# The first feed-forward block's up product as seven half-size products in one PSUM bank, with all places found anew

## The chip, the core and the metric

The kernel runs on one core of a Trainium2 chip. The metric is device time in microseconds (us) of one execution, the median of several runs. A core has five engines with a queue each, which run their own instructions in order and wait for one another by semaphores: TensorE (PE in the profile; PEld is its weight load), VectorE (DVE), ScalarE (ACT), GpSimd (POOL) and SyncE (SP), which here issues the DMAs. Matmuls read SBUF and write PSUM, which has eight banks.

## The reference, cut to what matters

For each of 64 graphs with 256 nodes and 256 features (all float32), a transformer layer on the graph is followed by two graph-attention layers and a second feed-forward block:

```python
# layer 0
x = ln(src + masked_attention(src) @ Wo + bo, g1, beta1)       # 8 heads
ff = gelu(x @ W1 + b1) @ W2 + b2                                # 256 -> 1024 -> 256: block "ffa"
x = ln(x + ff, g2, beta2)
# layer 1
h = gat(gat(x, adj, gW1, ga1), adj, gW2, ga2)
h = ln(x + h, g_ln1, b_ln1)
ff = relu(h @ w_ff1 + b_ff1) @ w_ff2 + b_ff2                    # block "ffb"
out = ln(h + ff, g_ln2, b_ln2)
```

The change concerns `x @ W1`, the up product of block `ffa`.

## The kernel before

All weights stay in SBUF. The work of one graph is cut into 210 named operations, each a method that emits one or a few instructions. A table `PLACES` gives each name a place in time, and graph g's operation stands at `g * PERIOD + place`; all operations of all graphs are emitted in the order of these places, under a schedule by hand that keeps this order on each engine:

```python
plan += [(g * PERIOD + t, i, ops[n]) for i, (n, t) in enumerate(PLACES.items())]
with tc.manual_schedule():
    for _, _, f in sorted(plan, key=lambda p: p[:2]):
        f()
```

The places only set an order; the engines run as fast as their waits allow. A graph's operations reach over more than five periods, so in the steady state up to six graphs are in work at once, and each engine goes through the same cycle of operations for each graph. `LOAD_PLACES` and the constants after it place the weights' loads and one-time preparations in the same order. Both tables come from a planner outside the kernel, of which only the places are here.

Names used below. `qk0`, `qk1`, `s0`, `s1`, `vp1` to `vp7`, `po0`, `po1`, `wo` are TensorE's products of attention (queries and keys, scores, values as seven half-size products, heads, output); `max`, `exp`, `rec`, `nrm`, `eT`, `pm` with two digits are softmax, transposition and masking of a half and a head; `qkc`, `oT`, `vc1` are ScalarE's copies out of PSUM; `va` VectorE's sums. `ga`, `ip`, `h1`, `h2` are TensorE's products of the graph attention; `gac`, `z`, `ze`, `zd`, `h1c` ScalarE's part (copy, scores, exponential, division, copy) and `zl`, `zm`, `zx`, `h2a` VectorE's (leaky step, mask, maximum, last add), with A or B for the two layers. `st`, `rt`, `nb`, `ln` and `lg`, `lb` are the layer norms: statistics on VectorE, root and offset on GpSimd, application on ScalarE, gain and shift on GpSimd. `tg` and `te` are one-column activations on ScalarE that bring the Gelu or the Exp table in.

A feed-forward block has the letter a or b: `aT`, `aW`, `aR` transpose the input in 32x32 squares on VectorE, write it to DRAM and read it back, the features then on the partitions; `au0` to `au3` (method `up`, line 408) each make 256 of the 1024 hidden features in one PSUM bank, four matmuls of 128x128 weights and 256 nodes:

```python
for f in range(f0, f0 + 2):
    for k in range(KD):
        nc.tensor.matmul(p[:, f - f0, :], self.wa[:, k, f * P:(f + 1) * P], self.x.nodes(k),
                         start=(k == 0), stop=(k == KD - 1))
```

`ax0` to `ax3` (method `act`, line 416) apply the function on ScalarE, two instructions each, from PSUM to SBUF. The down product is made of seven half-size products `ad1` to `ad7` (line 442) already, from differences `aS1` to `aS4` on GpSimd (line 431), summed up on VectorE by `ae`, `ae1`, `ae5`, `ae6`, `ae7` (line 450). `ag`, `ar` prepare the residual on GpSimd. Block b is alike and keeps its form.

PSUM is split into a pool `mm` of three banks that serves every product named above but the scores (four banks) and part of the down products (one bank).

TensorE's order in one period, from the graph attention's first product on:

```
ga1 ga0 bd2 ipA bd1 bd5 bd3 au3 bd6 bd4 au1 au0 h11 h10 au2 ipB bd7 s1 po0 ad3 ad2 ad5 ad1 vp1 ad4 ad7 h2
vp6 ad6 qk0 po1 vp7 vp2 wo vp5 qk1 vp4 s0 vp3 bu0 bu1 bu2 bu3
```

Of the kernel before, what the change touches and what calls it, by code (L numbers as in the profile page):

```python
# [9 lines left out]
F32 = mybir.dt.float32  # L10
# [5 lines left out]
ALU = mybir.AluOpType  # L16
AX = mybir.AxisListType

P = 128
S = 32  # L20
# [4 lines left out]

PERIOD = 46.817006
PLACES = {
    "te": 58.6001, "load": 103.4118, "xT": 107.5511, "qk0": 114.6030, "qkc0": 118.3668, "chk": 120.8735,  # L30
    "qk1": 124.1765, "qkc1": 125.7661, "s0": 125.8575, "max01": 128.7295, "max00": 129.3509, "exp00": 129.7832,
    "exp01": 131.1121, "max03": 131.1181, "rec00": 132.0400, "max02": 134.4535, "nrm00": 135.2195, "exp03": 135.2725,
    "exp02": 135.4496, "xS": 137.4219, "rec03": 139.9573, "rec01": 140.4767, "cast": 142.2696, "eT00": 146.3076,
    "nrm03": 146.9438, "rec02": 148.2727, "s1": 150.9705, "eT03": 153.2280, "eW00": 153.8592, "max10": 154.0476,
    "max12": 154.0810, "nrm01": 155.8608, "vp1": 157.2562, "eT01": 157.4751, "max11": 157.8791, "eW03": 157.8980,
    "exp10": 158.1195, "exp12": 158.3273, "rec10": 158.3689, "vc1": 159.1149, "nrm10": 159.7013, "exp11": 159.7336,
    "vp6": 160.5405, "y": 161.0091, "eR03": 162.4098, "jT": 162.4105, "va6": 163.4204, "eW01": 164.7326,
    "eT10": 167.2105, "vp7": 167.6555, "max13": 167.6890, "rec11": 168.1740, "rec12": 168.2052, "vp2": 170.1442,
    "va1": 170.6120, "va7": 170.6882, "nrm11": 170.8368, "vp5": 170.8550, "eW10": 171.9961, "exp13": 172.1818,
    "nrm12": 172.1818, "vp4": 172.3252, "nrm02": 172.3767, "rec13": 172.4280, "vb1": 172.4717, "nrm13": 172.8764,  # L40
    "va9": 173.2360, "vp3": 174.4288, "va5": 174.7560, "eT12": 175.2182, "eR00": 175.4819, "eT02": 175.4846,
    "va3": 175.9229, "va4": 176.3211, "eW02": 177.5999, "yb": 178.0406, "eT13": 179.1841, "eR01": 179.5795,
    "eT11": 181.3423, "eW12": 184.6438, "pm01": 187.1564, "pm03": 187.6323, "eR02": 190.0912, "eW11": 190.1738,
    "pm02": 191.4548, "vb0": 191.5291, "pm00": 196.1306, "eR12": 196.9971, "po0": 198.3305, "tg": 198.9884,
    "oT0": 203.0869, "pm12": 203.1747, "eW13": 203.2324, "eR11": 203.2324, "pm11": 204.4851, "eR10": 204.7143,
    "pm10": 205.0782, "eR13": 206.0478, "pm13": 210.8288, "po1": 212.8636, "oT1": 213.1603, "wo": 217.3657,
    "ya": 217.7482, "st1": 218.9733, "rt1": 219.6991, "nb1": 220.2046, "ln1": 221.5003, "aT": 223.1218,
    "aW": 223.5752, "aR": 228.4507, "au3": 233.0381, "au1": 235.4781, "ax3": 235.8335, "au0": 237.9132,
    "ax1": 237.9558, "ag": 239.9088, "ax0": 240.5771, "ar": 242.0854, "au2": 242.5252, "aS1": 243.4701,
    "ax2": 244.9981, "ad3": 245.3069, "aS2": 246.6456, "aS3": 246.8135, "ad2": 248.2816, "aS4": 248.9901,  # L50
    "ad5": 249.6928, "ad1": 250.8660, "ad4": 251.3076, "ad7": 251.4266, "ae": 251.5139, "ae1": 251.8960,
    "ae7": 253.0074, "ad6": 254.7553, "ae5": 256.3794, "ae6": 256.8974, "st2": 258.4200, "rt2": 261.8668,
    "nb2": 262.3317, "ln2": 262.5757, "lg2": 265.0579, "lb2": 265.2601, "hT": 266.8520, "hW": 269.2569,
    "hR": 270.2281, "no": 270.8009, "ga1": 272.1110, "gac1": 272.1189, "ga0": 272.2913, "gac0": 272.3261,
    "ipA": 275.0907, "zA": 275.3493, "zlA": 276.2527, "zmA": 279.1628, "zxA": 279.3183, "zeA": 279.6032,
    "zdA": 282.9918, "h11": 287.2020, "h10": 288.5186, "h1c0": 289.7363, "h1c1": 289.7594, "ipB": 290.9252,
    "zB": 291.0511, "zlB": 291.2329, "zmB": 292.8115, "zxB": 293.7145, "zeB": 297.0297, "zdB": 298.0214,
    "h2": 298.5319, "h2a": 302.0194, "st3": 302.9618, "rt3": 303.6799, "nb3": 304.4826, "ln3": 305.0823,
    "bT": 307.2531, "bW": 308.3438, "bR": 314.8880, "bu0": 316.1573, "bu1": 316.7829, "bx0": 316.9660,
    "bu2": 317.2893, "bx1": 317.6215, "bu3": 317.8128, "bx2": 318.1921, "bx3": 319.0641, "bS1": 319.5718,  # L60
    "bg": 319.6424, "bS2": 319.9853, "br": 320.8440, "bd2": 321.4268, "bd1": 322.8462, "bS4": 323.7921,
    "bS3": 324.5246, "bd5": 325.8209, "bd3": 325.8217, "bd6": 327.2744, "bd4": 327.8256, "be1": 328.2453,
    "be5": 329.8795, "be6": 331.7955, "be": 332.7084, "bd7": 337.7800, "be7": 342.4869, "st4": 344.9883,
    "rt4": 345.1762, "nb4": 348.7424, "ln4": 355.9706, "lg4": 361.3841, "lb4": 362.9841, "store": 364.6106,
}
LOAD_PLACES = [
    101.366, 142.216, 210.928, 179.882, 111.464, 161.951, 112.848, 100.995, 176.282, 144.653, 176.020, 153.991,
    122.933, 161.019, 117.691, 142.137, 176.282, 109.079, 176.294, 241.513, 253.083, 121.392, 182.287, 196.253,
    207.821, 129.075, 215.004, 184.114, 158.647, 204.480, 111.464, 207.869, 213.180, 214.956, 213.949, 222.383,
    259.685, 196.355, 250.874, 266.888, 159.287, 109.005, 208.310, 182.294, 221.373, 230.689, 234.043, 257.548,  # L70
    184.117,
]
V_PLACE, OUT_PLACE, FFA_PLACE, GAT_PLACE, FFB_PLACE, ODD_PLACE = 113.801, 158.647, 184.117, 225.125, 272.083, 240.000

# [11 lines left out]
def binary_graphs(  # L88
# [13 lines left out]
    nc = tc.nc  # L102
    B, N, D = x.shape
    R = 2
    FF = W1.shape[1]
    H = 8
    DH = D // H
    KD = D // P
    KF = FF // P
    C = N // P  # L110
# [15 lines left out]
    def mm_tile(shape, name, dt=F32):  # L126
        return ps_mm.tile(shape, dt, tag="mm", name=name)
# [42 lines left out]
    def rowvec(v, n, name):  # L170
        t = const.tile([P, n], F32, name=name)
        loads.append((t, _row(v, n)))
        return t
# [39 lines left out]
    wo, bo_r = weight(Wo, "wo"), rowvec(bo, D, "bo_r")  # L213
# [5 lines left out]
    g1_c, be1_c = mixed_vec(g1, "g1_c"), mixed_vec(beta1, "be1_c")  # L219
    w2, b2_r = weight(W2, "w2"), rowvec(b2, D, "b2_r")  # L220
    w2_t, f2_t = (const.tile([P, 3, KF // 2, P], F32, name=f"{n}_t") for n in ("w2", "f2"))
    g2_r, be2_r = rowvec(g2, D, "g2_r"), rowvec(beta2, D, "be2_r")
    gw = bp.tile([P, 2, KD, D], F32, tag="ff", name="gw", bufs=3)
    gw1 = gw[:, 0]
# [16 lines left out]
    def ffn_weights(w, b, gain, shift, row, shift_row, name, wb, wb_t):  # L241


        p = mm_tile([P, KF], f"{name}_b_ps")
        for f in range(KF):
            for k in range(KD):
                nc.tensor.matmul(p[:, f:f + 1], w[:, k, f * P:(f + 1) * P], shift[:, k],
                                 start=(k == 0), stop=(k == KD - 1))
        nc.vector.tensor_tensor(b, p, b, ALU.add)
        for k in range(KD):  # L250
            nc.scalar.activation(w[:, k], w[:, k], AF.Copy, scale=gain[:, k])
        nc.vector.tensor_tensor(row, row, shift_row, ALU.add)
        seven[name] = seven_weights([[wb[:, h * KF // 2:(h + 1) * KF // 2, d * P:(d + 1) * P] for d in range(2)]
                                     for h in range(2)], [wb_t[:, i] for i in range(3)])

    seven = {}

    def seven_weights(b, t):

# [126 lines left out]
    class Ffn:  # L386


        def __init__(self, wa, ba, func, wb, gain, row, name):
            self.wa, self.ba, self.func, self.wb, self.name = wa, ba, func, wb, name  # L390
            self.h, self.p = {}, {}
            self.gain, self.row = gain, row
            self.x = Transposed(f"{name}_T", bp, "sT", 2)
            self.ps = {}
            self.t = None

        def residual(self, src):
            self.r = bp.tile([P, C, D], F32, tag="res", name=f"{self.name}_res", bufs=3)
# [12 lines left out]
        def act(self, f0):  # L411
            half, f1 = divmod(f0, KF // 2)
            if half not in self.h:
                self.h[half] = bp.tile([P, KF // 2, N], F32, tag="ff", name=f"{self.name}_h{half}", bufs=3)
            for f in range(2):
                nc.scalar.activation(self.h[half][:, f1 + f, :], self.ps[f0][:, f, :], self.func,  # L416
                                     bias=self.ba[:, f0 + f:f0 + f + 1])

        def hidden(self, c, half):

# [31 lines left out]
    class Graph:  # L452
# [244 lines left out]
        def operations(self):  # L697
# [38 lines left out]
            for n, f, src in (("a", self.ffa, lambda: self.y), ("b", self.ffb, lambda: self.ffa.r)):  # L736
                ops[f"{n}T"] = lambda f=f, src=src: f.x.squares(src())
                ops[f"{n}W"], ops[f"{n}R"] = f.x.write, f.x.read
                ops[f"{n}g"] = lambda f=f, src=src: f.residual(src())
                ops[f"{n}r"] = f.residual_row  # L740
                for i in range(KF // 2):
                    ops[f"{n}u{i}"] = lambda f=f, i=i: f.up(2 * i)
                    ops[f"{n}x{i}"] = lambda f=f, i=i: f.act(2 * i)
                for i in range(1, 5):
# [303 lines left out]
```

## Time and profile before

| | |
|---|---|
| median of 3 runs | 3187.36 us (3186.81 to 3187.7) |
| the profiled execution: its time | 3185.44 us |
| its span, first to last instruction | 3183.7 us |
| TensorE matmul busy | 3076.2 us, 97% of the span |
| VectorE, ScalarE, GpSimd busy | 2377.3, 2328.3, 2196.3 us |
| up product of `ffa` (L408) | 2048 records, 475.8 us |
| its Gelus (L416) | 512, mean 473 ns, 214.8 us |
| down product's 128-wide matmuls, largest group (L442) | 1024 records, 139.6 us |
| mean granted clock of TensorE | 0.987 |

Busy time of a group is the time in which at least one of its instructions ran, so overlapping matmuls are not counted twice. A float32 matmul leaves two records. In a timeline a row gives start, length, engine, line, operation, `out<-in`, tile, shape and count, and in brackets the idle time of the engine before it with what ended it.

### The profile page before, as it was taken

The numbers are of one execution on the slowest core, as the hardware profiler recorded it, in microseconds if no ns is written. First come the engines' busy times: TensorE is split into PE (matmuls) and PEld (weight loads), VectorE is DVE, ScalarE is ACT, GpSimd is POOL, SyncE is SP. The second block draws the span as 40 slices with busy tenths as digits, with TensorE's granted clock in tenths as the row PEclk, the third lists the DMA queues.
The fourth block names the chain that finished last, engine by engine and source line by source line (L and its number), as shares of the span: only waits on it lengthen the run. The fifth ranks groups of instructions, "written<-read, shape, count | busy, mean of one in ns | idle before, by whom it ended". The sixth has DMA issues, their size and how long they took to land. (4 is left out here: it accounts for less than half of the span.)

```text
span 3183.7 us, 63717 instructions
## 1 busy us (share of the span) xinstructions
PE 3076.2 (97%) x21725; PEld 2588.3 (81%) x21725; DVE 2377.3 (75%) x5153; ACT 2328.3 (73%) x6599; POOL 2196.3 (69%) x2630
## 2 busy tenths in 40 slices
PE   6999999999999999999999999999999999999995
PEld 4788888888888888888888888888888888888784
DVE  5777777777777777777777777777777777777742
ACT  5777777777777777777777777777777777777742
POOL 2477677677677677677677677677677677677664
PEclk8999999999999999999999999999999999999997
DMA  7555455455455455555455455455455455455421
GB/s 207 155 151 144 141 156 144 140 156 145 140 156 144 140 156 145 140 156 145 140 156 145 140 155 146 140 153 148 140 154 147 139 154 147 139 154 148 133 70 31
DMA packets 808331, 456.62 MB, mean 143 GB/s; under 512 B 334528, under 2 KB 717376, under 8 KB 808000
## 3 DMA queue, kind: packets, MB, share of 16 engines
q1 hardware_dynamic: 808000, 452.49, 49.5%
q8 instruction: 174, 2.85, 0.4%
q14 instruction: 157, 1.29, 0.1%
HBM read 242.63 MB, written 201.33 MB: 139 GB/s over the span
## 5 line engine op out<-in xcount | busy, mean ns | idle before, releaser
L568 ACT ACTIVATE e<-e,rden 128x256 f32<-128x256 f32 x1024 | 455.8, 504 | 87.5 <-DVE rden L563 87.5
L408 PE MATMUL ffb_ps<-ffb_T,f 128*128 128x256 f32 x2048 | 461.6, 384 | 25.6 <-DMA ffb_T<-ffb_T_d 23.2
L408 PE MATMUL ffa_ps<-ffa_T,w 128*128 128x256 f32 x2048 | 475.8, 381 | 0.0
L558 ACT ACTIVATE e<-s,nmax 128x256 f32<-128x256 f32 x1024 | 470.0, 469 | 7.5 <-DVE nmax L550 6.9
L408 PEld LDWEIGHTS ffb_ps<-ffb_T,f 128*128 128x128 f32 x2048 | 392.8, 193 | 84.7 <-DMA ffb_T<-ffb_T_d 20.6
L577 DVE TENSOR_TENSOR pm<-eT,adT 128x512 f32<-128x512 f32 x512 | 436.7, 854 | 3.1 <-DMA eT<-eT_d 3.1
L326 DVE STREAM_TRANSPOSE eT_sq<-e 128x512 f32<-128x512 f32 x512 | 350.2, 693 | 107.2 <-DMA ffa_T_d<-ffa_T_sq 94.1
L408 PEld LDWEIGHTS ffa_ps<-ffa_T,w 128*128 128x128 f32 x2048 | 381.6, 191 | 47.9 <-ACT ffa_h L416 0.4
L373 POOL TENSOR_SCALAR rs_x<-mv_x 128x2 f32<-128x2 f32 x256 | 57.1, 223 | 451.7 <-DVE mv_x L369 444.3
L550 DVE TENSOR_REDUCE nmax<-s 128x2 f32<-128x512 f32 x512 | 335.6, 666 | 0.5 <-PE s L545 0.4
L416 ACT ACTIVATE ffb_h<-ffb_ps,bf_c 128x256 f32<-128x256 f32 x512 | 215.4, 473 | 122.5 <-PE ffb_ps L408 122.5
L384 ACT ACTIVATE ffa_res<-ffa_res,nb_x,rs_x 128x256 f32<-128x256 f32 x256 | 139.4, 593 | 191.6 <-POOL nb_x L379 191.5
L644 DVE SCALAR_TENSOR_TENSOR ga_z<-ga_z 128x512 f32<-128x512 f32 x64 | 88.4, 1381 | 233.3 <-ACT ga_z L641 233.3
L431 POOL TENSOR_TENSOR ffa_t<-ffa_h,ffa_t 128x512 f32<-128x512 f32 x128 | 165.6, 1294 | 130.8 <-ACT spare L692 123.5
L431 POOL TENSOR_TENSOR ffb_t<-ffb_h,ffb_t 128x512 f32<-128x512 f32 x128 | 191.3, 1494 | 89.5 <-ACT ffb_h L416 87.9
L416 ACT ACTIVATE ffa_h<-ffa_ps,b_c 128x256 f32<-128x256 f32 x512 | 214.8, 473 | 51.8 <-PE ffa_ps L408 50.7
L644 DVE SCALAR_TENSOR_TENSOR gb_z<-gb_z 128x512 f32<-128x512 f32 x64 | 44.3, 692 | 228.3 <-ACT gb_z L641 228.3
L558 ACT ACTIVATION_READ_ACCUMULATOR e<-s,nmax 128x1 f32 x1024 | 208.9, 204 | 0.0
L374 POOL TENSOR_TENSOR rs_x<-rs_x,nhalf 128x2 f32<-128x2 f32 x256 | 182.2, 712 | 21.3
L530 DVE TENSOR_TENSOR v<-v,v_ps 128x256 f32<-128x256 f32 x448 | 168.8, 399 | 0.4 <-PE v_ps L521 0.4
L351 POOL TENSOR_TENSOR ffa_res<-ffa_res,g_r 128x512 f32<-128x512 f32 x64 | 81.8, 1278 | 122.1 <-ACT ffa_res L384 122.1
L545 PE MATMUL s<-kT,qT 32*128 32x256 f32 x2048 | 149.9, 404 | 5.2 <-ACT e L558 5.2
(163 smaller groups left out, 8020.8 us busy)
## 6 DMA issues: line engine op xcount, KB each, us to landing
eT_d<-eT_sq SPq DMA_DIRECT2D x512, 256.0 KB, 2.9
eT<-eT_d SPq DMA_DIRECT2D x512, 256.0 KB, 3.4
xin<-in_x_dram SPq DMA_DIRECT2D x256, 64.0 KB, 3.1
adi<-in_adj_dram SPq DMA_DIRECT2D x64, 256.0 KB, 2.7
y<-in_x_dram SPq DMA_DIRECT2D x64, 256.0 KB, 4.3
ffa_T_d<-ffa_T_sq SPq DMA_DIRECT2D x64, 256.0 KB, 2.4
ffa_T<-ffa_T_d SPq DMA_DIRECT2D x64, 256.0 KB, 2.9
hT_d<-hT_sq SPq DMA_DIRECT2D x64, 256.0 KB, 2.0
```

What stands on the lines that cost most here:

```text
L326: nc.vector.transpose(self.sq.rearrange("p a c k y -> p (c k) a y"), src.rearrange("p c (k a x) -> p (c k) a x", k=KD, a=A))
L374: nc.gpsimd.tensor_tensor(self.rs, self.rs, nhalf, ALU.pow)
L384: nc.scalar.activation(yc, yc, AF.Identity, bias=self.nb[:, c:c + 1], scale=self.rs[:, c:c + 1])
L408: nc.tensor.matmul(p[:, f - f0, :], self.wa[:, k, f * P:(f + 1) * P], self.x.nodes(k), start=(k == 0), stop=(k == KD - 1))
L416: nc.scalar.activation(self.h[half][:, f1 + f, :], self.ps[f0][:, f, :], self.func, bias=self.ba[:, f0 + f:f0 + f + 1])
L431: nc.gpsimd.tensor_tensor(out, a, b, ALU.subtract)
L530: nc.vector.tensor_tensor(self.v_part(*to), self.v_part(*src), self.ps["v", i], ALU.add)
L545: nc.tensor.matmul(self.s4[m][h][:, ic * N:(ic + 1) * N], self.qT[hp, m, ic * P:(ic + 1) * P], self.kT[hp, m, :], start=True, stop=True)
L550: nc.vector.tensor_reduce(self.nmax[m, h], self.s4[m][h].rearrange("p (c n) -> p c n", c=C), AX.X, ALU.max, negate=True)
L558: nc.scalar.activation(e[:, ic, :], self.s4[m][h][:, ic * N:(ic + 1) * N], AF.Exp, bias=self.nmax[m, h][:, ic:ic + 1], accum_out=self.den[ ...
L568: nc.scalar.activation(e[:, ic, :], e[:, ic, :], AF.Copy, scale=self.rden[m, h][:, ic:ic + 1])
L577: nc.vector.tensor_tensor(self.pm[m, h].rearrange("p c k (b y) -> p (c k) b y", b=A), t.rearrange("p b c k y -> p (c k) b y"), self.adT.re ...
```

## The change

The product of block `ffa` is split in halves: 128 + 128 input features, 512 + 512 hidden features, 128 + 128 nodes. Seven products of half size `ap1` to `ap7` (four matmuls of 128 nodes each, method `up_part`) take the place of `au0` to `au3`. Their right sides are halves of the input or one of four differences `at1` to `at4` (GpSimd, method `node_sum`); their left sides are quarters of the weight or sums of them, made once in `ffn_weights` by four more adds on VectorE. `ap1`, `ap6`, `ap7`, `ap4` add up in one PSUM bank, bank 0 below, and after each of them ScalarE copies the whole bank, 128x512, into a quarter of the hidden tile (`ac1`, `ac6`, `ac7`, `ac4`, method `up_copy`). `ap2` goes to a second bank, `ap5` and then `ap3` to a third, and VectorE adds these to the quarters (`aa1`, `aa7`, `aa6`, method `up_add`). The Gelus then run in place in SBUF (`act_in_place`). The three banks come from the pool `mm`.

All places are new. TensorE's order in one period and ScalarE's:

```
ga0 ga1 bd2 ipA bd3 bd1 ap1 ap2 bd6 s1 ap6 h11 bd5 h10 ap7 ap5 ap4 bd4 ap3 ipB bd7 po0 vp1 ad3 ad5 ad1 ad2 ad7 ad4
h2 qk0 ad6 po1 vp7 vp6 wo vp5 vp3 s0 vp2 qk1 vp4 bu1 bu2 bu0 bu3

gac0 gac1 exp03 zA exp02 exp01 ac1 zeA zdA nrm03 ac6 h1c1 exp12 h1c0 ac7 tg ac4 ax2 zB ax1 ax0 ax3 nrm12 oT0 zeB vc1
zdB nrm01 exp10 exp13 ln4 nrm10 qkc0 exp11 ln3 oT1 nrm02 nrm13 ln2 qkc1 exp00 te ln1 bx1 bx2 nrm00 bx0 nrm11 bx3
```

```diff
-PERIOD = 46.817006
+PERIOD = 46.802000
...
-    "aW": 223.5752, "aR": 228.4507, "au3": 233.0381, "au1": 235.4781, "ax3": 235.8335, "au0": 237.9132,
-    "ax1": 237.9558, "ag": 239.9088, "ax0": 240.5771, "ar": 242.0854, "au2": 242.5252, "aS1": 243.4701,
...
+    "no": 243.1288, "at1": 243.2863, "at2": 243.3266, "ap1": 243.3672, "ap2": 243.9675, "ac1": 244.5699,
+    "aa1": 245.3645, "ap6": 245.5386, "at3": 245.5532, "ac6": 247.4691, "at4": 247.9916, "ap7": 249.4691,
+    "ar": 250.1780, "ap5": 250.3386, "ac7": 251.1468, "ap4": 251.5565, "aa7": 252.0569, "tg": 252.3489,
+    "ap3": 252.4143, "ac4": 252.8450, "ax2": 253.7964, "aa6": 254.2113, "ax1": 256.9508, "ax0": 257.6471,
...
-V_PLACE, OUT_PLACE, FFA_PLACE, GAT_PLACE, FFB_PLACE, ODD_PLACE = 113.801, 158.647, 184.117, 225.125, 272.083, 240.000
+V_PLACE, OUT_PLACE, FFA_PLACE, GAT_PLACE, FFB_PLACE, ODD_PLACE = 133.293, 191.755, 242.862, 282.414, 309.485, 240.000
...
+    up_t = {n: const.tile([P, 3, FF // 2], F32, name=f"{n}_u") for n in ('ffa',)}
...
+        if name in up_t:
+            (a11, a21), (a12, a22) = ([w[:, k, i * FF // 2:(i + 1) * FF // 2] for i in range(2)] for k in range(KD))
+            s1, s2, s4 = (up_t[name][:, i] for i in range(3))
+            nc.vector.tensor_tensor(s1, a21, a22, ALU.add)
+            nc.vector.tensor_tensor(s2, s1, a11, ALU.subtract)
+            nc.vector.tensor_tensor(s4, a12, s2, ALU.subtract)
+            nc.vector.tensor_tensor(a21, a11, a21, ALU.subtract)
+            up_w[name] = {1: a11, 2: a12, 3: s4, 4: a22, 5: s1, 6: s2, 7: a21}
...
+        def node_sum(self, i):
+            if self.xt is None:
+                self.xt = bp.tile([P, 4, P], F32, tag="us", name=f"{self.name}_xt", bufs=1)
+            (b11, b12), (b21, b22) = ([self.x.nodes(k)[:, j] for j in range(C)] for k in range(KD))
+            t = [self.xt[:, j].rearrange("p (b y) -> p b y", y=S) for j in range(4)]
+            o, a, b = {1: (t[0], b12, b11), 2: (t[1], b22, t[0]), 3: (t[2], b22, b12), 4: (t[3], b21, t[1])}[i]
+            nc.gpsimd.tensor_tensor(o, a, b, ALU.subtract)
+
+        def up_part(self, i):
+            bank = {1: 0, 6: 0, 7: 0, 4: 0, 2: 1, 5: 2, 3: 2}[i]
+            if bank not in self.ps:
+                self.ps[bank] = mm_tile([P, KF // 2, P], f"{self.name}_ps{bank}")
+            whole = {1: (0, 0), 2: (1, 0), 3: (1, 1)}
+            if i in whole:
+                k, j = whole[i]
+                b = self.x.nodes(k)[:, j]
+            else:
+                b = self.xt[:, {5: 0, 6: 1, 7: 2, 4: 3}[i]]
+            w = up_w[self.name[:3]][i]
+            for f in range(KF // 2):
+                nc.tensor.matmul(self.ps[bank][:, f], w[:, f * P:(f + 1) * P], b, start=(i in (1, 2, 5) and f == 0),
+                                 stop=(f == KF // 2 - 1), skip_group_check=True)
+
+        def half_of(self, i, j):
+            if i not in self.h:
+                self.h[i] = bp.tile([P, KF // 2, N], F32, tag="ff", name=f"{self.name}_h{i}", bufs=3)
+            return self.h[i][:, :, j * P:(j + 1) * P]
+
+        def up_copy(self, i):
+            nc.scalar.copy(self.half_of(*{1: (0, 0), 6: (0, 1), 7: (1, 1), 4: (1, 0)}[i]), self.ps[0])
+
+        def up_add(self, i):
+            bank, to = {1: (1, (0, 0)), 7: (2, (1, 1)), 6: (2, (0, 1))}[i]
+            t = self.half_of(*to)
+            nc.vector.tensor_tensor(t, self.ps[bank], t, ALU.add)
+
+        def act_in_place(self, f0):
+            half, f1 = divmod(f0, KF // 2)
+            for f in range(2):
+                h = self.h[half][:, f1 + f, :]
+                nc.scalar.activation(h, h, self.func, bias=self.ba[:, f0 + f:f0 + f + 1])
...
+                if f.name[:3] in up_t:
+                    for i in range(1, 5):
+                        ops[f"{n}t{i}"] = lambda f=f, i=i: f.node_sum(i)
+                    for i in range(1, 8):
+                        ops[f"{n}p{i}"] = lambda f=f, i=i: f.up_part(i)
...
```

## Prediction, written before the changed kernel ran

> **What bounds the kernel now.** I read the busy shares first, then a stretch of the steady state, then TensorE's timeline in one period, then what the other engines do where TensorE waits.
>
> The page's first part and its slices (one digit per fortieth of the span, tenths):
>
> ```profile
> PE 3076.2 (97%) x21725; PEld 2588.3 (81%) x21725; DVE 2377.3 (75%) x5153; ACT 2328.3 (73%) x6599; POOL 2196.3 (69%) x2630
> PE   6999999999999999999999999999999999999995
> PEclk8999999999999999999999999999999999999997
> ```
>
> TensorE is full from the second slice to the last but one, at full granted clock; a 400 us stretch has it busy for 395.55 us. The other four sit at 69 to 81%. So a microsecond of TensorE work is worth a microsecond, if no wait replaces it. TensorE's timeline (start, length with the pipeline's tail, operation, records) gives the prices; each matmul leaves two records:
>
> ```profile
> 1507.13 1.89 PE L408 MATMUL ffa_ps<-ffa_T,w 128*128 128x256 f32 x8
> 1508.86 1.05 PE L442 MATMUL ffb_po<-f_t,ffb_t 128*128 128x128 f32 x8
> 1509.75 1.06 PE L442 MATMUL ffb_pq<-f,ffb_t 128*128 128x128 f32 x8
> 1510.65 3.62 PE L408 MATMUL ffa_ps<-ffa_T,w 128*128 128x256 f32 x16
> 1514.10 1.90 PE L669 MATMUL h_ps<-ga_wh,ga_z 128*128 128x258 f32 x8
> ...
> 1530.05 1.05 PE L442 MATMUL ffa_po<-w_t,ffa_t 128*128 128x128 f32 x8
> ...
> 2964.42 1.05 PE L442 MATMUL ffa_po<-w_t,ffa_t 128*128 128x128 f32 x8
> ```
>
> Starts, not lengths, are what counts: four 256-wide matmuls occupy 1508.86 - 1507.13 = 1.73 us, four 128-wide ones 1509.75 - 1508.86 = 0.89 us. The last two rows are the same step 30 graphs apart: the period is 1434.37 / 30 = 47.81 us. Summing starts over one period, matmul work is 45.9 us (126 256-wide records at 0.216, 116 128-wide ones at 0.112, scores 2.1, attention products 3.6); the other 1.9 us are waits and the 0.1 us that each change between 32-row or 32-column and full tiles costs.
>
> Where a period waits most, on TensorE and on ScalarE:
>
> ```profile
> 1534.63 0.70 PE L521 MATMUL v_ps<-wv,xs 128*128 128x256 f32 x2
> 1535.62 0.70 PE L521 MATMUL v_ps<-wv,xT 128*128 128x256 f32 x2 [0.29 <-ACT kT L508]
> ```
>
> ```profile
> 1533.76 1.09 ACT L384 ACTIVATE ffa_res<-ffa_res,nb_x,rs_x 128x256 f32<-128x256 f32 x2 [2.81 <-POOL nb_x L379]
> 1535.47 0.36 ACT L598 COPY oT<-po 128x256 f32<-128x256 f32 x1
> ```
>
> ScalarE idles 2.81 us until GpSimd has the offset of `ln3`; `qkc0` and `oT1` queue behind it, and TensorE's `vp2` starts 0.99 us after `vp7` where 0.43 would do: 0.56 us lost.
>
> **The change, part by part.**
>
> *TensorE.* Removed: four `up` steps of four 256-wide matmuls, 4 x 1.73 = 6.92 us. Added: seven steps of four 128-wide ones, 7 x 0.893 = 6.25 us. Saved: 0.67 us per graph, on the bound engine. Not one eighth: a half-size step costs more than half a whole one.
>
> The row for a 128-wide stream with a new weight for each matmul is 0.89 us for eight records, 112 ns each. The Trainium skill, "TensorE: Matmul & The Clock Gate", section "Back-to-back issue gap", speaks against this: it gives 55.6 ns for an isolated 128-column pass but some 81 ns in a stream of weight loads and matmuls. With two passes to a record, 56 records would take, as an estimate from that page, 56 x 162 ns = 9.1 us and the change would lose 2.1 us per graph. The down product's rows decide: 112 ns.
>
> *ScalarE.* Four copies of 128x512 from PSUM are added. The nearest rows are 128x260 copies at 381 ns (L628) and the growth from 256 to 1024 columns on L251 and L568, (1142 - 504) / 768 = 0.83 ns per column: 0.37 + 256 x 0.83 = 0.58 us; bounds 0.38 and two short copies, 0.76. Eight Gelus read SBUF instead of PSUM: 504 against 473 ns, 0.03 each (norm rows at 593 ns would make it 0.12). Sum 2.6 us on an engine with 36.4 us of work per graph.
>
> *VectorE.* Three 128x512 adds of PSUM and SBUF, priced by `ya` (L616, 692 ns): 2.1 us on 37.1. *GpSimd.* Four 128x128 differences at 610 to 666 ns (L475): 2.6 us on 34.3. Neither comes near 47, so they cost something only where a successor waits.
>
> *The waits added.* In the emitted order each product that adds into bank 0 waits for ScalarE's copy before it: p1, copy, p6, copy, p7, copy, p4, copy. Other work must fill these gaps, and no row of this trace shows one, so the order has to be walked. I walk the emitted order with start-to-start times from the timeline, zero at the second `ga` product:
>
> TensorE: ap1 3.8, ap2 4.7, bd6 5.5, s1 6.5, ap6 7.6, h11 8.6, bd5 9.5, h10 10.3, ap7 11.2, ap5 12.1, ap4 13.0, bd4 13.9, ap3 14.8, ipB 15.7, bd7, po0, vp1, ad3 19.2, ad5 20.1, ad1, ad2, ad7 22.8, ad4 23.7, h2 24.6, qk0 26.3, ad6, po1 29.0, vp7, vp6, wo 31.9.
>
> - ScalarE before ac1: exp03, zA, exp02, exp01 end at 4.8; ac1 4.85 to 5.4. ap6 at 7.6 has 2 us to spare.
> - zeA 5.5 (after zA, leaky step, mask and maximum of 0.7 to 1.4 + 0.8 + 0.7 us), zdA to 7.7 or 8.4: h11 at 8.6 just fits; queued behind on ScalarE: nrm03, ac6 to 9.2, h1c1 to 10.0, exp12, h1c0 to 11.8. ap7 (11.2) and ap5 (12.1, it needs h10's bank) fit by 0.3.
> - ap7's last matmul ends at 12.3, ac7 at 12.9, ap4 wants 13.0: a tie, 0.1 us. Behind ac7 stand the Gelu table load (1283 ns) and ac4 to 14.9; only ipB (15.7) needs that bank.
> - ax2 15.7, zB, ax1, ax0 to 18.5, ax3 to 19.3. ad3 reads ax3's half from 19.6. GpSimd's aS1, aS3, aS2, aS4 run 18.6 to 23.6 (4 x 1.25); ad4 wants 23.7: a tie.
> - The Exp table load now stands directly ahead of zeB (20.4), instead of under VectorE's work: zeB to 22.6, reciprocal, zdB to 24.0. h2 wants 24.6.
> - h2 ends at 26.5; add, statistics, offset and ln3 take what they take in the trace (1529.79 to 1534.75: 5.0 us), plus 0.5 us behind lg4 on GpSimd: 32.1; oT1 then to 32.4. wo waits 0.5 us. This is the old 0.56 us wait at `vp2` in a new place: nothing won or lost.
> - bT's write and read took 5.0 us (1535.62 issue, 1537.67 read, 2.9 to land); 5.8 remain before bu1. hT, aT and the load places on SP keep at least 1 us; I cost them at nothing, and at 0.5 us per period if an earlier queue entry holds them.
>
> Sum per graph: -0.67; tile-mode changes, since s1 no longer adjoins po0, +0.18; ties at ap4, ad3, ad5, ad4, h11, +0.3; the waits of the old `ffa_pq` steps (1521.71 to 1524.78: 3.07 us where 2.68 would do) go, -0.38. That is -0.57: a period of 47.24 us. Some 60 full periods: -34 us. At the ends: the last graph has nothing to put between product and copy, three hand-overs of about 0.75 us and two slower Gelu pairs, +2.6 us, up to +8 with the longer pipeline; the weights' sums are four adds (4 x 0.69 us) once, ahead of the first use. I take +8 together. Net -26 us: 3185.44 to 3159.4 in the profiled execution, which is 1.9 us under the median of 3187.36; in those terms 3161.
>
> **Rivals.**
>
> *A, the hand-overs eat it.* About seven steps on TensorE now wait for an engine that ended just before; the trace charges about 0.09 us for such a start (1538.39 - 1537.88 is 0.51 for a 0.43 us step). Seven of them are the saving: period 47.7 to 47.9, total 3183 to 3201. For it: the ties above. Against it: half of them have over 0.5 us of cover.
>
> *B, ScalarE becomes late: slower.* From ac7 to zdB ScalarE has no gap, with 0.6 us of cover before h2; ln3, oT1 and wo follow h2. If copies cost 0.76, Gelus the norm's 593 ns and zB or the Exp load slip by half a microsecond, h2 is 1.6 us late, 1.0 past the cover: period 48.2, +23 + 8, total 3218. It decides from 0.6 us late onward, and loses from 1.2. Against it: each price is the far bound.
>
> *C, better packing.* wo's wait vanishes because lg4 is early, and the ties don't show: period 46.8 to 46.9, -58 + 6, about 3137.
>
> **How the numbers follow.** Forecast 0.50 (3150 to 3174), C 0.13, A 0.17 (half of it within 0.2%), B 0.20. About 0.2%, 6.4 us, is what a measurement of this kernel can tell from no change. Faster 0.63, same 0.09, slower 0.28. The range runs from C's 3136 to 3205, leaving out most of B.
>
> **What would show it.** Right: up products in 0.89 us each, starts 47.2 us apart, copies near 0.58 us, no idle row at ap6, ap7 or ap4 beyond 0.1 us, `wo` waiting for oT. Wrong: TensorE idle until a copy of `ffa_ps`, or h2 until `gb_wh`; a 128x512 copy over 0.76 us; or a span whose period falls while the time doesn't, which puts the cost into the ends.

## The result, and the profile after

| | before | changed |
|---|---|---|
| median of 8 runs each | 3185.58 us (3181.9 to 3187.7) | 3195.13 us (3193.6 to 3196.96) |
| ratio, 95% interval | | 1.0031 (1.002 to 1.0042) |
| the profiled execution: time, span | 3185.44, 3183.7 us | 3193.6, 3191.7 us |

The change makes the kernel slower by 0.3%. The forecast was 3161 us and faster; the time lies inside the range, on the other side of no change.

The page of the changed kernel, its first part and slices, then the groups the forecast had priced (engine, operation, shape, count, busy time, mean ns of one, idle time before and what ended most of it):

```profile
PE 3050.3 (96%) x23261; PEld 2626.8 (82%) x23261; DVE 2521.3 (79%) x5349; ACT 2479.2 (78%) x6853; POOL 2336.9 (73%) x2886
...
PE   6899999999999999999999999999999999999985
...
L476 ACT ACTIVATE ffa_h<-ffa_h,b_c 128x256 f32<-128x256 f32 x512 | 217.7, 501 | 2.2
...
L490 POOL TENSOR_TENSOR ffa_t<-ffa_h,ffa_t 128x512 f32<-128x512 f32 x128 | 195.1, 1524 | 5.0
...
L464 ACT COPY ffa_h<-ffa_ps 128x512 f32<-128x512 f32 x256 | 148.8, 581 | 41.3 <-PE ffa_ps L453 40.8
L490 POOL TENSOR_TENSOR ffb_t<-ffb_h,ffb_t 128x512 f32<-128x512 f32 x128 | 163.4, 1277 | 21.0 <-ACT ffb_h L428 20.8
...
L470 DVE TENSOR_TENSOR ffa_h<-ffa_ps,ffa_h 128x512 f32<-128x512 f32 x192 | 131.5, 685 | 42.3 <-PE ffa_ps L453 42.2
```

TensorE is still full in 36 slices of 40, but it is busy for 26 us less than before while the span is 8 us longer. The prices of the new copies, Gelus and adds are as forecast. One row is not: GpSimd's differences `aS2` and `aS4` of block a, 1524 ns each, where the same operation on the same shape in block b takes 1277. In the page of the kernel before it is the other way round, and that was there to be read:

```profile
L431 POOL TENSOR_TENSOR ffa_t<-ffa_h,ffa_t 128x512 f32<-128x512 f32 x128 | 165.6, 1294 | 130.8 <-ACT spare L692 123.5
L431 POOL TENSOR_TENSOR ffb_t<-ffb_h,ffb_t 128x512 f32<-128x512 f32 x128 | 191.3, 1494 | 89.5 <-ACT ffb_h L416 87.9
```

So the operation has two prices, and what stands beside it must decide which one is paid. In the trace before, the 63 slowest of block b, 1.73 us each, begin while VectorE's leaky step `zlA` runs, which has both inputs in SBUF, and end 1.13 to 1.14 us after it.

TensorE's timeline in one steady period of the changed kernel: `ap1` and `ap2`, `ap6`, `ap5`, `ap4`, `ap3`, then `ad7` and `ad4`:

```profile
1514.87 1.95 PE L453 MATMUL ffa_ps<-ffa_T,w 128*128 128x128 f32 x16
...
1518.72 1.16 PE L453 MATMUL ffa_ps<-ffa_xt,ffa_u 128*128 128x128 f32 x8
...
1523.24 1.06 PE L453 MATMUL ffa_ps<-ffa_xt,ffa_u 128*128 128x128 f32 x8
1524.13 1.16 PE L453 MATMUL ffa_ps<-ffa_xt,w 128*128 128x128 f32 x8
...
1526.02 1.06 PE L453 MATMUL ffa_ps<-ffa_T,ffa_u 128*128 128x128 f32 x8
...
1534.09 1.06 PE L501 MATMUL ffa_po<-w,ffa_h 128*128 128x128 f32 x8
1536.01 1.16 PE L501 MATMUL ffa_pq<-w,ffa_t 128*128 128x128 f32 x8 [0.86 <-POOL ffa_t L490]
```

No up product has an idle row before it; `ap6` and `ap4` take 0.99 and 1.00 us from start to start, the others 0.89. The one idle row of the period stands at `ad4`, which waits for `aS4`: it starts 1.92 us after `ad7`, where 0.89 would do.

GpSimd there, `aS1`, `aS3`, then `aS2` and `aS4` in one row:

```profile
1529.89 1.28 POOL L490 TENSOR_TENSOR ffa_t<-ffa_h 128x512 f32<-128x512 f32 x1 [4.33 <-DVE gb_z L706]
1531.25 1.60 POOL L490 TENSOR_TENSOR ffa_h<-ffa_h,ffa_h 128x512 f32<-128x512 f32 x1
1532.82 3.14 POOL L490 TENSOR_TENSOR ffa_t<-ffa_h,ffa_t 128x512 f32<-128x512 f32 x2
```

And VectorE's two masked products `pm10` and `pm12` (products of a transposed half with the mask, both inputs in SBUF) in the same microseconds:

```profile
1530.81 0.91 DVE L636 TENSOR_TENSOR pm<-eT,adT 128x512 f32<-128x512 f32 x1
...
1534.13 0.69 DVE L636 TENSOR_TENSOR pm<-eT,adT 128x512 f32<-128x512 f32 x1
```

The two kinds exclude each other. `pm10` starts within `aS1`, which ends at 1531.17, and ends at 1531.72, 0.55 us after it; `aS3`, begun meanwhile, takes 0.32 more than `aS1` and ends 1.13 us after `pm10`. `aS2`, at 1.27, ends at 1534.09; `pm12` starts at 1534.13 and `aS4` 0.03 us behind it; `aS4` takes 1.79 us, again to 1.13 us after `pm12`. It is so in the whole trace: the 180 masked products that begin within a difference (of either block) end 0.54 to 0.58 us after it, whether they last 0.68 or 1.78 us; all 125 differences of over 1.4 us begin within a masked product, and only 3 of the other 387 do. From 1529.89 to 1535.96 the four differences take 6.07 us; the forecast had 5.0.

Where the 8 us of span are, by the starts of `wo`: the fourth graph's comes 10.8 us later than before (208.54 against 197.74), the next 59 graphs take 5.5 us less (2814.0 against 2819.5), the rest 2.7 us more. Most periods are 47.65 us long (47.80 before; a few irregular ones lift the mean to 47.70). Over those 59 graphs TensorE's idle rows are 0.90 us a graph, 0.47 before; what is left, its own work with the small stalls inside, is 46.80 us, 47.32 before. So of 0.52 us saved, 0.43 became a wait.

### The profile page after: what moved, and what is told of

Its sections match the earlier page's. It is cut to its first block, busy times and chain, and to the rows that moved or that the text cites. A ratio compares the mean times of both kernels' runs of the same rounds, so it can differ in the third digit from the quotient of the medians.

```text
span 3191.7 us, 67685 instructions
## 1 busy us (share of the span) xinstructions
PE 3050.3 (96%) x23261; PEld 2626.8 (82%) x23261; DVE 2521.3 (79%) x5349; ACT 2479.2 (78%) x6853; POOL 2336.9 (73%) x2886
## 5 line engine op out<-in xcount | busy, mean ns | idle before, releaser
L565 ACT ACTIVATE qT<-qk_ps,bqs_c 128x256 f32<-128x256 f32 x128 | 60.7, 474 | 306.5 <-PE qk_ps L556 306.4
L490 POOL TENSOR_TENSOR ffa_t<-ffa_h 128x512 f32<-128x512 f32 x64 | 81.8, 1279 | 292.4 <-DVE gb_z L706 258.8
L476 ACT ACTIVATE ffa_h<-ffa_h,b_c 128x256 f32<-128x256 f32 x512 | 217.7, 501 | 2.2
L386 POOL TENSOR_TENSOR rs_x<-rs_x,nhalf 128x2 f32<-128x2 f32 x256 | 200.7, 784 | 21.3
L490 POOL TENSOR_TENSOR ffa_t<-ffa_h,ffa_t 128x512 f32<-128x512 f32 x128 | 195.1, 1524 | 5.0
L490 POOL TENSOR_TENSOR ffb_t<-ffb_h 128x512 f32<-128x512 f32 x64 | 82.0, 1281 | 156.5 <-ACT ffb_h L428 156.5
L464 ACT COPY ffa_h<-ffa_ps 128x512 f32<-128x512 f32 x256 | 148.8, 581 | 41.3 <-PE ffa_ps L453 40.8
L490 POOL TENSOR_TENSOR ffb_t<-ffb_h,ffb_t 128x512 f32<-128x512 f32 x128 | 163.4, 1277 | 21.0 <-ACT ffb_h L428 20.8
L509 DVE TENSOR_TENSOR ffb_res<-ffb_po,ffb_res 128x256 f32<-128x256 f32 (+2 forms) x256 | 132.9, 519 | 53.0 <-issue 24.0
L470 DVE TENSOR_TENSOR ffa_h<-ffa_ps,ffa_h 128x512 f32<-128x512 f32 x192 | 131.5, 685 | 42.3 <-PE ffa_ps L453 42.2
```

Of the source, the lines that this page charges most:

```text
L386: nc.gpsimd.tensor_tensor(self.rs, self.rs, nhalf, ALU.pow)
L476: nc.scalar.activation(h, h, self.func, bias=self.ba[:, f0 + f:f0 + f + 1])
L490: nc.gpsimd.tensor_tensor(out, a, b, ALU.subtract)
```

## The experiments

Each was timed beside the kernel before (medians from 3185.1 to 3186.4 us); the ratio is to it. "Idle" is the sum of TensorE's idle rows (0.15 us and longer) per graph over 59 graphs, as above; "period" is the length of most periods.

| kernel | median, us | ratio (95% interval) | period, us | idle, us |
|---|---|---|---|---|
| before | 3185.6 | | 47.80 | 0.47 |
| changed | 3195.1 | 1.0031 (1.002 to 1.0042) | 47.65 | 0.90 |
| e6_ad2_longer | 3198.3 | 1.0039 (1.0026 to 1.0053) | 47.66 | 0.24 |
| e1_ad4_later | 3173.5 | 0.9964 (0.9951 to 0.9978) | 47.26 | 0.49 |
| e8_pm_behind | 3161.9 | 0.9930 (0.9913 to 0.9946) | 47.12 | 0.31 |
| e7_oT_first | 3170.1 | 0.9951 (0.9935 to 0.9968) | 47.23 | 0.54 |
| e9_oT_first_ad2_longer | 3190.0 | 1.0015 (1.0005 to 1.0024) | 47.53 | 0.30 |
| e16_pm_behind_oT_first | 3166.7 | 0.9937 (0.9923 to 0.995) | 47.13 | 0.33 |
| e17_pm_behind_ad2_longer | 3168.2 | 0.9948 (0.9933 to 0.9963) | 47.19 | 0.03 |
| e13_before_qkc0 | 3170.0 | 0.9954 (0.9937 to 0.997) | 47.56 | 0.38 |

### Is TensorE's saving lost in ad4's wait?

```diff
 # Ffn.down
+            again = 3 if i == 2 and self.name[:3] in up_t else 0
+            for _ in range(again):
+                nc.tensor.matmul(self.p[bank][:, k], a[:, 0], seven[self.name[:3]][i][:, 0], start=True, stop=True)
```

> The first matmul of ad2 is issued three times more (each begins the sum anew), 3 x 0.223 = 0.67 us of TensorE work per graph, as much as the seven products save; it stands just ahead of ad7 and ad4. Theory (in the changed kernel TensorE waits there for ScalarE's Gelus and GpSimd's differences, so the saved time is idle time): it costs under 0.1 us per period, under 6 us in all. Rival (TensorE is still the bound all along the period): +0.67 us per period, +41 us, 3236.

Measured: 3.1 us more than the changed kernel, for 42 us of matmul work; the theory held. The waits of TensorE for `aS4`, of the changed kernel and of this one, whose lines stand three further down (total us, times, longest):

```profile
PE ffa_pq L501 <- POOL ffa_t L490: 53.0, 62, 0.9
```

```profile
PE ffa_pq L504 <- POOL ffa_t L490: 11.9, 60, 0.2
```

The extra work sits inside the wait: `ad4` starts when GpSimd is done, whatever TensorE does just before. It doesn't say that time saved in the up products, further ahead, would be free too.

### Taking the wait away by TensorE's order

```diff
-"ad4": 265.6786, "ae": 265.7449, "ad6": 268.6987
+"ad4": 268.6987, "ae": 268.7100, "ad6": 265.6786
```

> The places of ad4 and ad6 are exchanged and ae is moved behind ad4; nothing else. Theory (the saved matmul time is lost in one wait per period: ad4 starts 1.92 us after ad2/ad7 where 0.89 would do, because it needs the last of four differences on GpSimd): the wait goes, the period falls from 47.65 to 46.6 to 46.8 us, the time from 3195 to 3131 to 3145. Rival 1 (the order as a whole is bound by a cycle through ScalarE and GpSimd, the wait only shows up there): the period stays above 47.4, time above 3180. Rival 2 (the loss is in the ends alone): no change of more than 5 us.

Measured: 21.6 us less than the changed kernel, and 0.36% under the kernel before. The wait at `ad4` is gone, but only half of it came back as time: 47.26 us lies between the theory's 46.8 and the first rival's 47.4. A period's idle row is now at `wo`:

```profile
1484.46 1.99 PE L671 MATMUL wo_ps<-wo,oT 128*128 128x256 f32 x8 [0.44 <-ACT oT L657]
```

`oT1` stands behind `ln3` on ScalarE, and `ln3` waits 1.23 us for GpSimd's offset of norm 3.

### Taking the wait away by VectorE's order

First try, with `pm10` and `pm12` put ahead of `aS1`:

```diff
-"eR12": 211.7882, "pm10": 212.6028, "pm12": 214.4221
+"eR12": 204.3629, "pm10": 207.3128, "pm12": 209.9121
```

> Two of VectorE's mask products, pm10 and pm12, are moved ahead of the leaky step of the second attention layer (with the read eR12 that pm12 needs), so that they no longer run beside GpSimd's aS3, aS2, aS4. Theory (GpSimd's 128x512 differences take 1.57 to 1.60 us instead of 1.28 because VectorE reads two SBUF operands at the same time): the three take 1.27 to 1.35 us, aS4 ends about 1 us earlier, ad4's wait falls below 0.2 us, the period to 46.6 to 46.9 and the time to 3131 to 3150. Rival (these differences are slow for another reason, such as their strided operands): they stay above 1.5 us, the period stays within 0.2 us of 47.65.

Measured: 3491.26 us, ratio 1.0958, far slower. VectorE's and GpSimd's rows:

```profile
1670.95 0.69 DVE L636 TENSOR_TENSOR pm<-eT,adT 128x512 f32<-128x512 f32 x1 [3.29 <-PE po L651]
```

```profile
1674.11 1.28 POOL L490 TENSOR_TENSOR ffa_t<-ffa_h 128x512 f32<-128x512 f32 x1 [7.73 <-DVE gb_z L703]
1675.46 1.26 POOL L490 TENSOR_TENSOR ffa_h<-ffa_h,ffa_h 128x512 f32<-128x512 f32 x1
1676.69 2.62 POOL L490 TENSOR_TENSOR ffa_t<-ffa_h,ffa_t 128x512 f32<-128x512 f32 x2
```

The edit overlooked that `pm` has four buffers, which `po0` frees: VectorE, in order, stood still for 3.29 us a graph with everything behind it, and TensorE's mean granted clock was 0.946, where the changed kernel had 0.986. But the differences, with no masked product beside them, took 1.28, 1.26 and 2.62 us.

Second try, behind `eT12`, where `aS4` is nearly done:

```diff
-"pm10": 212.6028, "pm12": 214.4221
+"pm10": 216.2080, "pm12": 216.3080
```

> The changed kernel with only pm10 and pm12, two VectorE products with two SBUF inputs, moved behind eT12, where GpSimd's last difference of block a is nearly done; TensorE's order is that of the changed kernel. Theory (those two hold up aS3 and aS4, and ad4 with them): the four differences take 5.1 to 5.2 us instead of 5.96, ad4's wait of 0.86 us shrinks to 0.1 or less, period 46.9 to 47.1, about 3152 us (3145 to 3165). Rival (GpSimd's times are its own, or the delayed products of VectorE make ae, h2a and oT1 late instead): differences at 1.6 us each, or a wait at wo of 0.5 us or more; period 47.4 or more, over 3178 us.

Measured: 33 us less than the changed kernel, 0.7% under the kernel before; the theory held. It has the lowest median of the study, though e14 and e16 below lie within its interval. GpSimd:

```profile
1511.79 1.27 POOL L490 TENSOR_TENSOR ffa_t<-ffa_h 128x512 f32<-128x512 f32 x1 [4.35 <-DVE gb_z L706]
1513.14 1.28 POOL L490 TENSOR_TENSOR ffa_h<-ffa_h,ffa_h 128x512 f32<-128x512 f32 x1
1514.37 2.63 POOL L490 TENSOR_TENSOR ffa_t<-ffa_h,ffa_t 128x512 f32<-128x512 f32 x2
...
1522.09 0.56 POOL L385 TENSOR_SCALAR rs_x<-mv_x 128x2 f32<-128x2 f32 x1
1522.74 1.00 POOL L386 TENSOR_TENSOR rs_x<-rs_x,nhalf 128x2 f32<-128x2 f32 x1
```

Over all graphs the group's mean falls from 1524 to 1283 ns:

```profile
L490 POOL TENSOR_TENSOR ffa_t<-ffa_h,ffa_t 128x512 f32<-128x512 f32 x128 | 164.3, 1283 | 5.0
```

TensorE, `ad7`, `ad4` and the next graph's `wo`:

```profile
1515.99 1.06 PE L501 MATMUL ffa_po<-w,ffa_h 128*128 128x128 f32 x8
1517.06 1.16 PE L501 MATMUL ffa_pq<-w,ffa_t 128*128 128x128 f32 x8
...
1525.78 1.99 PE L671 MATMUL wo_ps<-wo,oT 128*128 128x256 f32 x8 [0.29 <-ACT oT L657]
```

In this period the four differences take 5.21 us instead of 6.07: the 0.86 us are as long as the idle row that is gone. TensorE's starts in a period, counted from `wo`, agree with the changed kernel's within 0.02 us up to `ad7` (37.34 and 37.33), and then `ad4` follows after 1.07 us instead of 1.92. So it is VectorE's two products, not GpSimd's own time, that made `ad4` wait. The period's 47.12 us lie below the forecast's 47.24.

The last two GpSimd rows are the root of norm 3, beside `pm11` and `pm13`. The same steps take 0.22 and 0.71 us in norms 1 and 2, and 0.55 and 1.02 in norm 4, which `pm10` and `pm12` now stand beside. TensorE waits 0.29 us at `wo`, at the end of norm 3's chain.

### What bounds it next

Further attempts on the wait at `wo`, and some kernels that lengthen TensorE's part; none is faster than e8_pm_behind.

```diff
 # e7: e1_ad4_later and
-"oT1": 225.7544, "ln3": 316.3769
+"oT1": 223.6084, "ln3": 317.4125
```

> The changed kernel with ad4 and ad6 exchanged as in e1_ad4_later, and ScalarE's oT1 put ahead of ln3. In e1_ad4_later a period is 47.26 us, of which TensorE idles 0.44 us at wo, until oT1 is there; oT1 stands on ScalarE behind ln3, which waits 1.23 us for GpSimd. Theory (the change is worth its matmul time, 0.5 us per graph, once no product waits): the 0.44 us go, period 46.8 to 46.9, 3173.5 less 60 x 0.4 = about 3148 us (3142 to 3156). Rival (another wait takes the place, since ln3 and all that follows it come 0.3 us later): period 47.1 or more, over 3163 us.

Measured: 3.5 us less than e1_ad4_later; the rival held. VectorE's transposition for block b follows `ln3`, the sums of the values follow it, and TensorE waits for the last of those:

```profile
1491.96 7.17 PE L420 MATMUL ffb_ps<-ffb_T,f 128*128 128x256 f32 x32 [0.51 <-DVE v L589]
```

```diff
 # e9: e7_oT_first and, in Ffn.down
+            again = 3 if i == 2 and self.name[:3] in up_t else 0
+            for _ in range(again): ...
```

> e7_oT_first with the three extra matmuls of e6_ad2_longer in ad2 (their results are overwritten by the next one): 0.67 us more TensorE work per graph, the amount that the seven products save against the four whole ones. In the changed kernel's order this cost 3.1 us. Theory (in e7_oT_first TensorE bounds every period): now it costs 63 x 0.6 to 0.67 = 38 to 42 us over e7_oT_first. Rival (a chain outside TensorE still bounds): under 20 us.

Measured: 20 us more than e7_oT_first, half of TensorE's 42 us, on the edge of the rival's range. Idle rows fall by 0.24 us a graph, so part of the added work took the place of waits; TensorE alone did not bound the period.

```diff
 # e16: e8_pm_behind and
-"oT1": 225.7544, "ln3": 316.3769
+"oT1": 223.6084, "ln3": 317.4125
```

> e8_pm_behind with oT1 ahead of ln3 on ScalarE. In e8_pm_behind TensorE waits 0.29 us of a 47.12 us period at wo, for oT1 behind ln3. Theory (with pm10 and pm12 gone from the differences, VectorE is 0.9 us earlier at bT than in e7_oT_first, against wo, so the later ln3 costs it less): the 0.29 us go and at most 0.2 come back where bu waits for the sums of the values; period 46.85 to 47.05, 3148 to 3158 us. Rival (VectorE's sums take all of it, as in e7_oT_first): 47.1 or more, 3160 us or more.

Measured: the period stays at 47.13; the 0.29 us at `wo` became 0.26 at block b's up product, again for VectorE's sums. The rival held.

```diff
 # e17: e8_pm_behind and, in Ffn.down
+            again = 3 if i == 2 and self.name[:3] in up_t else 0
+            for _ in range(again): ...
```

> e8_pm_behind with the three extra matmuls of e6_ad2_longer in ad2 (their results are overwritten), 0.67 us of TensorE work per graph. In the changed kernel they cost 3.1 us, all the rest hidden under ad4's wait. Theory (with that wait gone, ad2, ad4, h2, ln3, oT1, wo are one chain through TensorE): 0.55 to 0.67 us per period, 33 to 42 us over e8_pm_behind, so 3195 to 3204 us. Rival (another engine's round through the period is nearly as long): under 20 us.

Measured: 6.3 us more than e8_pm_behind; the theory fell. The added 0.67 us lengthen the period by 0.07, and next to no idle row is left. In e8_pm_behind VectorE runs without a gap from 1516.03 (`eT12`) to `h2a` at 1520.32, 0.38 us after `h2` is done; 1.51 us of this stretch are the two masked products that e8 put there; so `h2a`, `ln3` and `oT1` follow VectorE, and TensorE has some 0.6 us to spare between `ad2` and `wo`.

```diff
 # e11: e8_pm_behind and
-"pm11": 220.8456, "pm13": 220.8464, "ae": 265.7449, "ae1": 265.8658, "ae7": 266.1487
+"pm11": 218.9080, "pm13": 218.9090, "ae": 267.6100, "ae1": 267.6110, "ae7": 267.6120
```

> e8_pm_behind with the other two masked products of that half, pm11 and pm13, taken out from beside GpSimd's root of norm 3: they stand behind pm12 now, ahead of h2a, and ae, ae1, ae7 behind st3. In e8_pm_behind a period is 47.12 us, 0.29 of it TensorE waiting at wo for oT1, which stands behind ln3, which waits for that root; the root's two steps take 0.56 and 1.00 us beside pm11 and pm13 and 0.22 and 0.71 without. Theory (the same blocking of GpSimd by these VectorE products holds wo): the two steps fall to 0.22 and 0.72, the wait at wo goes, period 46.83 to 46.9, 3161.9 less 17 = about 3145 us (3140 to 3152). Rival (another wait takes its place): period over 47.0, over 3155 us.

Measured: 3252.3 us, ratio 1.0205, period 48.52. The root's two steps fell to 0.22 and 0.71 as both sides had it, but the rival held, harder than thought:

```profile
1570.50 1.16 PE L501 MATMUL ffa_po<-w_t,ffa_t 128*128 128x128 f32 x8 [1.69 <-DVE ffa_res L509]
```

`ad6` writes the PSUM bank that `ae1` and `ae7` read; both were put too late. e12 added the three extra matmuls to this and so does not test what it was meant to:

```diff
 # e12: e11_pm11_13_early and, in Ffn.down
+            again = 3 if i == 2 and self.name[:3] in up_t else 0
+            for _ in range(again): ...
```

> e11_pm11_13_early with the three extra matmuls of e6_ad2_longer in ad2 (their results are overwritten), 0.67 us of TensorE work per graph. Theory (TensorE bounds each period now, so the seven products' saving counts in full): 0.6 to 0.67 us per period more, 38 to 42 us over e11_pm11_13_early. Rival (a chain outside TensorE is as long): under 25 us. In the changed kernel it cost 3 us, in e7_oT_first 20.

Measured: 3278.18 us, ratio 1.0289, 26 more than e11, just past the rival's 25, with the same wait of 1.69 us.

```diff
 # e14: e1_ad4_later and
-"pm11": 220.8456, "pm13": 220.8464
+"pm11": 216.2580, "pm13": 216.2680
```

> e1_ad4_later (ad4 and ad6 exchanged, so that the four differences on GpSimd may be late) with pm11 and pm13 taken from beside norm 3's root to a place behind eT12, where VectorE waits for ScalarE; pm10 and pm12 stay beside the differences. Theory (GpSimd blocked by those two products holds ln3, then oT1, then wo, which waits 0.44 us in e1_ad4_later): the root's two steps fall from 0.54 and 1.01 us to 0.22 and 0.72, the wait at wo to 0.15 or less, period 46.9 to 47.0, 3173.5 less 15 to 20 = about 3156 us (3150 to 3162). Rival (VectorE's adds come late instead, as in e11_pm11_13_early): another wait of TensorE, period 47.2 or more, over 3170 us.

Measured: 3166.37 us, ratio 0.9936 (0.992 to 0.9953), period 47.15. The root of norm 3 falls to 0.22 and 0.71 us, but now norm 4's root takes 0.55 and 1.02, VectorE reaches `h2a` later, and `wo` waits 0.59 us, not less. The time is between the two, the mechanism nearer the rival's.

### The ends

```diff
 # e2
-LOAD_PLACES[4, 5, 7, 10, 11, 12, 14, 15] = 221.650, 221.641, 228.780, 234.573, 232.294, 235.866, 215.936, 228.515
+LOAD_PLACES[4, 5, 7, 10, 11, 12, 14, 15] = 140.1, 140.2, 151.0, 151.1, 151.2, 151.3, 130.2, 130.3
-FFA_PLACE = 242.862
+FFA_PLACE = 191.8
```

> Only the one-time preparation of block ffa's weights, and the loads that it needs, stand about one period earlier, at 191.8 instead of 242.9. Theory (the changed kernel loses some 11 us between the first and the third graph's output product because this preparation, 4.5 us of small matmuls, its sums on VectorE and two waits of 3.8 and 3.4 us, moved behind the first graph's attention): the third graph's output product starts at 150 to 153 us instead of 160.9, the period stays 47.65, the time falls by 8 to 11 us to about 3185 to 3187. Rival (the graph attention's weights or the order in general fill the start): less than 3 us.

Measured: 3203.93 us, ratio 1.0061 (1.0047 to 1.0074); the fourth `wo` at 218.3 us instead of 208.5. The theory missed: the first `wo` itself came 12 us later.

```diff
 # e10
-LOAD_PLACES[27, 29] = 259.336, 270.022; GAT_PLACE = 282.414
+LOAD_PLACES[27, 29] = 240.100, 240.200; GAT_PLACE = 243.0
```

> The changed kernel with the one-time preparation of the graph attention's weights, and its last two small loads, moved from between the second and third wo to just ahead of the first ap1, where TensorE idles 3.83 us for block a's input. Theory (the ends' loss of some 11 us comes from one-time work put where nothing else waits to be done): the start of the fourth wo comes 3 to 7 us earlier, 3188 to 3192 us in all. Rival (VectorE is the bound there, with the sums of weights): no change or later, 3195 to 3200 us.

Measured: 3201.97 us, ratio 1.0053 (1.0036 to 1.007), the fourth `wo` at 216.0. The rival's reason held, its size did not: from 75.8 to 82.9 us VectorE works on sums of weights and of a bias without a gap, and TensorE waits for the copy behind them:

```profile
83.65 1.87 PE L309 MATMUL gu_ps<-a2c,gw 128*128 128x2 f32 x8 [9.45 <-DVE gw L302]
```

```diff
 # e15, ffn_weights
-            nc.vector.tensor_tensor(s1, a21, a22, ALU.add)
-            nc.vector.tensor_tensor(s2, s1, a11, ALU.subtract)
-            nc.vector.tensor_tensor(s4, a12, s2, ALU.subtract)
-            nc.vector.tensor_tensor(a21, a11, a21, ALU.subtract)
-            up_w[name] = {1: a11, 2: a12, 3: s4, 4: a22, 5: s1, 6: s2, 7: a21}
+            up_w[name] = {1: a11, 2: a12, 3: a12, 4: a22, 5: a21, 6: a22, 7: a21}
```

> The changed kernel without the four one-time adds of weight quarters on VectorE (3.1 us in e10_gat_early's timeline); ap3, ap5, ap6 and ap7 read plain quarters, so these products are not the reference's. Theory (in the ramp VectorE has no gap after the weights, so each added microsecond delays the first graph): 2 to 4 us less than the changed kernel, 3191 to 3193 us, the fourth wo 2 to 4 us earlier. Rival (the ramp's loss comes from where the one-time work stands, not from how much there is): within 1 us of the changed kernel, the fourth wo within 1 us of 208.5.

Measured: 3194.33 us against the changed kernel's 3195.13, which overlap; the fourth `wo` at 206.3, 2.3 us earlier. By that start the theory held, by the time the rival. One trace does not settle it: in e8, e1, e17 and e6, whose weights stand as in the changed kernel, the fourth `wo` starts anywhere from 206.0 to 210.4 us. What the sums cost stays open, up to about 2 us of the 10.8.

### The kernel before with one wait mended

```diff
-"qkc0": 118.3668
+"qkc0": 117.7340
```

> The kernel before with one place changed: qkc0 ahead of ln3 on ScalarE, where it need not stand behind ln3's wait of 2.81 us for GpSimd. It tells what mending a wait is worth without the change. Theory (0.29 us of the 47.80 us period are TensorE waiting at vp2 for kT): period 47.5, 17 us less, about 3168 us (3163 to 3174). Rival (oT1 or the sums of the values take the place of it): period 47.7 or more, over 3178 us.

Measured: 16.3 us less than the kernel before beside it (3186.35). The theory held: `vp2`'s wait is gone, and `vp5` waits 0.36 us for VectorE's sums. So one moved place is worth 16 us to the kernel before. With one mended wait each, the seven products lead by 8 us (3161.9 against 3170.0), with ratio intervals that just overlap; and the changed kernel's is the best of several mended orders, the other's the only one made. That the seven products are faster is not shown.

## Why the prediction was wrong

**The step that failed** is "GpSimd's aS1, aS3, aS2, aS4 run 18.6 to 23.6 (4 x 1.25); ad4 wants 23.7: a tie". The order and the start were right (18.8 on that scale); the term of 5.0 us was 6.07, because two of the differences stood behind VectorE's masked products: without these they take 5.21, so 0.86 us is the exclusion, which the walk left out, and 0.2 the price. The sum charged all ties together with 0.3 us; this one cost 0.86 of idle time. With only the two masked products moved, the period fell by 0.53 us, to 0.12 under the forecast. The Trainium skill, "SBUF — State Buffer", section "Who interferes with whom", has the rule: a VectorE instruction with two SBUF inputs and a GpSimd instruction that reads SBUF exclude each other, and the second to issue waits for the whole of the first. The rows above agree with it: the later of the two ends a fixed 0.55 or 1.13 us after the earlier. The 1494 and 1294 ns of one operation in the page before were its sign.

**The saving**: -0.67 and -0.38 were to leave, +0.18 to come. The `ffa_pq` waits did go: `ad3` to `ad7` start 0.89 us apart (1530.52 to 1534.09 for four). The seven products take 6.45 us from start to start, not 6.25, with 0.10 at `ap6` and at `ap4`. In all TensorE's part fell by 0.52 us. That holds stalls under 0.15 us, so the forecast beside it is -0.87 and the 0.3 for ties, -0.57: near, as a sum; its parts were not all taken apart. What the forecast missed in a period is the idle rows, which it kept as long as before and which grew by 0.43 us.

**Prices**: copies 581 ns for 0.58 us, Gelus 501 for 504, adds 685 for 692, node differences 450 to 470 for 610 to 666; these two were means over mixed durations as well, the medians before are 458 and 461. The 112 ns for a record held: `ap1` and `ap2`, 16 records, start 1.79 us before the next step. The estimate of 162 ns from the Trainium skill's "TensorE: Matmul & The Clock Gate", section "Back-to-back issue gap", would have made that 2.6, which the trace does not bear out.

**Walk**: `ap6`, `ap7`, `ap4`, `ad3`, `h11` and `h2` wait 0.1 us or nothing, as walked; the Exp table load before `zeB` did not delay `h2`, which follows `ad4`. `wo` starts 0.13 us after it could, not 0.5; but in e8_pm_behind, where `ad4` no longer waits, it starts 0.45 late. So the walk had this wait right, and `ad4`'s wait hid it.

**Ends**: +8 was forecast and +13.5 came (10.8 and 2.7). Weight sums are at most some 2 us of it. Between the second and third `wo` 55.1 us pass where it was 47.2: the one-time products of the graph attention now stand there with the second block's. Moving one-time work alone made it worse twice; the cause of the rest stays open.

**Rivals**: by its numbers the result is A (period 47.7 to 47.9, 3183 to 3201 us), but its reason, about 0.09 us at each of seven hand-overs, is not what happened: two cost that (`ap6`, `ap4`), four nothing that shows, and one ten times as much. So A's numbers came out by luck. B did not occur: ScalarE was never late for `h2`. Of C, `wo`'s wait did go, but a tie showed (and its sum, -58 + 6, gives 3135, not 3137). Of the 34 us between forecast and result, 28 lie in the 59 steady graphs (-34 forecast, -5.5 measured) and 5.5 at the ends.

## What to carry to other kernels

When one operation on one shape has two mean durations in a profile, find out what stands beside the slow one before pricing a chain by the fast one; a tie in a walk is an open question, to be costed at its slow price. On a nearly full engine, saved time turns into whatever is next: here a wait in GpSimd, then VectorE's order, each within half a microsecond of the other in a 47 us period. And before calling a rewritten step good or bad, mend the largest idle row of both versions: one such mend was worth 33 us to the changed kernel and 16 to the one before, where the two differed by 9.5.

## What the hardware showed unexpectedly

- VectorE's 128x512 product with two SBUF inputs takes 0.64 to 0.69 us alone and up to 1.78 where a GpSimd difference was running: it ends 0.55 us after the difference, whenever it began. The difference takes 1.28 us alone, 1.60 and 1.79 where such a product had come first. The profile shows no idle time for this; the delay lies inside the busy time of the later instruction.
- Size doesn't protect: GpSimd's 128x2 steps take 0.22 and 0.71 us, and 0.56 and 1.00 beside these products. They carry a chain to `wo`.
- 0.67 us of matmuls more in each graph cost 3 us in all in one order, 6 in another, 20 in a third and 26 in a fourth.
